# One-hot rows of the tail lists from broadcast row lists, weighted ones on VectorE, and a POOL copy after every sixth gather

## The chip, the cores and the metric

The kernel runs on one core of a Trainium2 chip. The metric is the device time of one execution in microseconds (us); lower is better. The kernel before took a median of 753.49 us over eight runs (747.69 to 759.23).

The core's engines are TensorE (PE in the profile; its weight loads are PEld), VectorE (DVE), ScalarE (ACT), GpSimd (POOL) and SyncE (SP). Each takes its own instructions strictly in order. SP, ACT and POOL also issue DMA transfers; such an issue stands in the same order as the engine's other instructions.

## The reference

Two graph layers over 4096 nodes with 64 features, and a dense 4096 x 4096 matrix `adj` of zeros and ones in which a row holds eight ones on average:

```python
h = relu(layernorm(x))
x = x + layer0(h, adj)
h = relu(layernorm(x))
x = x + layer1(h, adj)
```

Layer 0 takes, for each node i, the mean over its neighbours j of a logarithmic map from i to j on the Poincare ball. The map needs the vectors h[i] and h[j], their norms, the norm of their difference, and an arctanh. A matrix product and an exponential map follow. Layer 1 is `w @ (h @ weight) + bias`, where `w` weighs the last neighbour of a row with 1, the one before it with 1/2, and so on: 0.5 to the power of the number of ones to its right in its row.

## The kernel before, in words

The kernel takes the sparse matrix apart instead of working on all pairs. Its nodes lie in 32 blocks of 128 rows; eight blocks are a quarter.

*The load stage.* SP loads `adj` in halves of a block into `room`; TensorE transposes it (L888), ACT writes it as small numbers into `masks` (L891), and TensorE packs it into words from which VectorE reads the columns of the ones (`pack`, `search`). The first six entries of a row's list, the ELL list, go to `ell_i`. What is left of all rows of a block is gathered into a compact tail list (`tail_split`, `tail_first`, `tail_second`). It holds three columns of 128 entries per block, and of each entry two things: the neighbour's number in `tail_i`, and the row within the block that it belongs to, counted from 1, in `tail_r` (0 for an empty entry). These four functions work per quarter and send their lists through memory on ACT's DMA queue to bring them into another layout.

*The units.* Layer 0 is worked off in 17 units. A unit has the ELL lists of two blocks (12 columns), or the tail lists of two or three blocks (6 or 9 columns), or both (up to 21). Units 0 to 4 have no tail, the last has nothing else; twelve have one. For a unit:

- `fetch` loads the blocks' own rows (`hi`) and, for a tail, the blocks' vectors as three bf16 parts (`hr`), on ACT's queue.
- `gather` has POOL issue one indirect DMA per column (L1139): 128 rows of 65 numbers from `tab_d` into the tile `g`, of which there are two.
- `tail_rows` makes, for a tail, the 0/1 matrix that says which row of its block each entry belongs to. ACT makes it in the orientation "entry by row" with one `Abs` per column (L1156) and one `Relu` (L1163), into `oh`. TensorE transposes it (L1169), and ACT copies it from PSUM into `mt` (L1170). With `mt` as weights and `hr` as data, TensorE selects for each entry its own row's vector (L1178) into a PSUM tile `sel` (and `mi` from the seventh column on).
- `differ` has VectorE subtract (L1192 for ELL, L1208 for the tail) into `d`, and ACT squares the result into `g` (L1222).
- `weigh` sums the squares on VectorE (L1234), after which `g` is free, and works out a weight `r` per entry on VectorE and ACT (L1235 to L1251).
- `total` multiplies the ELL part by `r` and adds it up on VectorE (L1281, L1288). For the tail, ACT scales the columns of `oh` by `r` into `mr` (L1261) and TensorE multiplies `mr` with `d` (L1266), again into a PSUM tile `sel`; `total_tail` adds that to `y` (L1295).

`mt` and `hr` share the memory of `mr`. There is one buffer each of `mr`, `oh`, `d`, of the PSUM tile `sel` and of `mi`, and two of `g` and `hi`.

*The rest.* `middle` finishes layer 0 for a group of blocks and makes the data of layer 1; `collect` has TensorE multiply `masks` with it (L1422, 1024 matmuls) and adds the results to `acc`, on VectorE (L1441, L1445) or through ACT and POOL (L1436, L1438). `write` sends `acc` out. A dense path at the end runs only where a list overflows; it is not entered here.

*What sets the order.* Each call is entered in `plan` with a time in us by `at`, and the times, less the offsets in `EARLY`, become priorities. A scheduler then fixes the order of every engine's instructions by these priorities and by its own account of when each could run; the semaphores are set by it, too. So an instruction need not stand where the program text has it. In `plan`, `tail_rows` is due 6 us after the unit's `gather`, `differ` 7.

Of the kernel before, what the change touches and what calls it, by code (L numbers as in the profile page):

```python
# [19 lines left out]
P = 128  # L20
# [28 lines left out]
QB = 8  # L49
# [7 lines left out]
TB = 3  # L57
MAXT = 3
# [490 lines left out]
def kernel(  # L549
# [61 lines left out]
    ta_d = [dram.tile([P, SUB], F32, name=f"ta_d{q}") for q in range(NQ)]  # L611
    flag_d = dram.tile([1, 1], I32, name="flag_d")
# [3 lines left out]
    with ExitStack() as fast:  # L616
# [67 lines left out]
        tail_i = const.tile([P, NB, TB], I32, name="tail_i")  # L684
        tail_r = const.tile([P, NB, TB], F32, name="tail_r")
# [64 lines left out]
        prep = fast.enter_context(tc.tile_pool(name="prep", bufs=2))  # L750
# [24 lines left out]
        nc.vector.tensor_scalar(pk[:, 1, :], f_e, pd_i.bitcast(F32), None, ALU.mult)  # L775
        row_i = late2[:, 2 * NG : 2 * NG + P].bitcast(I32)
# [39 lines left out]

        def expanded():
# [13 lines left out]
        gp = fast.enter_context(tc.tile_pool(name="gp", bufs=2))  # L831
        blk = fast.enter_context(tc.tile_pool(name="blk", bufs=1))
# [10 lines left out]
        EARLY = {"middle":30,"search":30,"fetch_words":30,"tail_rows":30,"differ":30,"weigh":30,"total":30,"total_tail":30,"ell_lists":30,"tail_split":30,"tail_first":30,"tail_second":30,"gather":30,"fetch":30}  # L843
# [210 lines left out]
        def tail_first(q):  # L1054
# [14 lines left out]
            tac = lst.tile([P, 4, SUB // 4], F32, name="tac")  # L1069
# [9 lines left out]
        def tail_second(q):  # L1079
# [20 lines left out]
            lt = lst.tile([32, REST], F32, name="lt")  # L1100
            nc.vector.transpose(lt, tb)
            lv = lt.rearrange("p (t k b) -> p k b t", t=TB, k=4)
# [9 lines left out]
        def fetch(u):  # L1112
            rb = u["ell"]
            if rb is not None:
                hi = blk2.tile([P, 2, DT], F32, name="hi")
                u["hi"] = hi[:, :, 1:DT]
                nc.scalar.dma_start(out=hi, in_=tab_v[:, rb : rb + 2, :])
            if u["tail"]:
                t0, nt = u["tail"]

                u["mr"] = blk.tile([P, MAXT * TB, P], F32, name="mr")
                half = u["mr"].rearrange("p b c -> p (b c)").bitcast(BF16)
                u["mt"] = half[:, 0 : MAXT * TB * P].rearrange("p (b c) -> p b c", c=P)
                hr = half[:, MAXT * TB * P :][:, 0 : MAXT * 3 * DT]
                u["hr"] = hr = hr.rearrange("p (b c) -> p b c", c=3 * DT)
                nc.scalar.dma_start(out=hr[:, 0:nt, :], in_=hp_d[:, t0 : t0 + nt, :])

        def gather(u):
# [9 lines left out]
            for k, i in enumerate(idx):  # L1138
# [5 lines left out]
                )  # L1144
            u["ns"] = len(idx)

        def tail_rows(u):

            if not u["tail"]:
                return  # L1150
            t0, nt = u["tail"]
            nb = nt * TB
            oh = u["oh"] = blk.tile([P, MAXT * TB, P], BF16, name="oh")

            for k in range(nb):
                nc.scalar.activation(  # L1156
                    oh[:, k, :],
                    row128,
                    AF.Abs,
                    bias=tail_r[:, t0 + k // TB, k % TB : k % TB + 1],  # L1160
                    scale=-1.0,
                )
            nc.scalar.activation(oh[:, 0:nb], oh[:, 0:nb], AF.Relu, bias=1.0, scale=-1.0)  # L1163
            mt, u["sel"] = u["mt"], []
            for k0 in range(0, nb, SEL):
                part = range(k0, min(k0 + SEL, nb))
                mp = ps_m.tile([P, SEL, P], BF16, name="mi")
                for k in part:
                    nc.tensor.transpose(mp[:, k - k0, :], oh[:, k, :], ident_b)  # L1169
                nc.scalar.copy(mt[:, k0 : part.stop], mp[:, 0 : len(part)])  # L1170
# [82 lines left out]
        def total(u):  # L1253
# [3 lines left out]
            if u["tail"]:  # L1257
                t0, nt = u["tail"]
                mr = u["mr"]
# [332 lines left out]
```

## Time and profile before

The profile is one execution, recorded by the hardware.

| | |
|---|---|
| time of the profiled execution | 757.62 us |
| its span, first to last instruction | 755.8 us |
| mean granted TensorE clock | 0.679 of full speed |
| gathers, POOL L1139 | 288, about 1.25 us apart within a train |
| `room` loads from `adj`, SP | 128 of 512 KB |
| `tl_d`, `ta_d` and their loads back, ACT's queue | 40 |

A row of a group names line, engine, operation, the output and input tiles with shapes and how often; then busy us and mean ns of one; then the idle time of the engine just ahead of these instructions, and what ended it. The chain that ended last is followed back from the last instruction, each time to what released it. "Issue" is time in which an engine waited for nothing that the profile shows; "remote", or "another core or an unknown queue", is a wait whose end the profile can put down to none of the core's engines or transfers. A run of gathers with no more than the usual 0.3 us between them is called a train here.

### The profile page before, as it was taken

Reading aid. Unit: us, or ns where it says so; the run is one execution under the profiler, and the core shown is the slowest. Engines: PE = TensorE matmul, PEld = TensorE weight load, DVE = VectorE, ACT = ScalarE, POOL = GpSimd, SP = SyncE. Lnnn points to the kernel's source line nnn. Section 1 sums busy time; section 2 is a strip of 40 time slices with the busy share of each in tenths; the row PEclk is TensorE's granted clock in tenths of the full one; section 3 lists DMA queues with packets and bytes.
Section 4 is the critical chain, followed back from the end, with each engine's and each line's share of the span. In section 5 each row is a group of like instructions: output and inputs, shape, how many; then the busy total and the mean of one; then the engine's idle time right before and its main releaser. Section 6 shows DMA issues by size and latency. Waiting matters only on the chain.

```text
span 755.8 us, 11841 instructions
## 1 busy us (share of the span) xinstructions
PE 395.0 (52%) x4094; PEld 338.3 (45%) x4094; DVE 404.0 (53%) x1557; ACT 345.1 (46%) x791; POOL 351.6 (47%) x423
## 2 busy tenths in 40 slices
PE   3651555624641607655067251442275368979881
PEld 3541444523531506554054241332164167979871
DVE  7750568635691607983179553793623136764520
ACT  6741655725660709955166251442242214565430
POOL 1285414255277260373705364577173712007892
PEclk9865568657775658956556555555556678998996
DMA  8983568746773616876201111221111110000001
GB/s 307 384 317 79 195 212 270 267 140 205 253 283 82 191 23 238 286 253 192 32 16 19 26 34 23 45 37 26 29 27 33 28 16 12 14 10 1 2 27 35
DMA packets 42858, 88.23 MB, mean 117 GB/s; under 512 B 14756, under 2 KB 20388, under 8 KB 42660
## 3 DMA queue, kind: packets, MB, share of 16 engines
q1 hardware_dynamic: 21458, 72.93, 26.9%
q0 software_dynamic: 9504, 10.67, 8.2%
q10 hardware_dynamic: 11826, 3.78, 2.2%
q8 instruction: 34, 0.56, 0.3%
q14 instruction: 36, 0.29, 0.1%
HBM read 83.11 MB, written 4.24 MB: 116 GB/s over the span
## 4 chain that ended last, share of the span: by engine, by line
DVE 23%; PE 21%; another core or an unknown queue 21%; ACT 16%; issue 11%; DMA 4%; ACTq 2%; POOL 1%; DVEq 0%; POOLq 0%; SPq 0%
PE a_ps L1422 9%; ACT mask L891 7%; PE a_ps L888 4%; DVE mask L1412 3%; PE words L917 2%; PE sel L1266 2%; DVE cand L981 1%; DVE tl L1095 1%; DMA room<-in_adj 1%; DVE tb L1093 1%; ACT oh L1156 1%; POOL acc L1438 1%; ACT mr L1261 1%; DMA w_sb<-in_L_gnn_weight 1%
## 5 line engine op out<-in xcount | busy, mean ns | idle before, releaser
L1139 POOL DMA_INDIRECT g<-tab_d,ell_i x192 | 199.6, 1039 | 268.6 <-DVE d L1234 72.3
L891 ACT ACTIVATE mask<-a_ps 128x1024 fp8e5<-128x1024 bf16 x128 | 128.0, 1028 | 111.2 <-remote 73.9
L888 PE MATMUL a_ps<-ident_b,room 128*128 128x128 bf16 x1024 | 103.8, 266 | 59.6 <-ACT mask L891 38.6
L1422 PE MATMUL a_ps<-room,mask 128*128 128x192 bf16 x1024 | 109.6, 259 | 34.2 <-issue 27.6
L888 PEld LDWEIGHTS <-room 128*128 128x128 bf16 x1024 | 90.0, 157 | 66.9 <-issue 66.5
L1139 POOL DMA_INDIRECT g<-tab_d,tail_i x96 | 93.4, 973 | 48.8 <-issue 27.4
L1422 PEld LDWEIGHTS <-mask 128*128 128x128 fp8e5 x1024 | 92.9, 104 | 44.3 <-issue 42.4
L917 PE MATMUL words<-pk,mask 128*128 128x64 bf16 x1024 | 59.3, 216 | 68.3 <-ACT mask L891 43.7
L917 PEld LDWEIGHTS <-mask 128*128 128x128 fp8e5 x1024 | 47.6, 113 | 100.5 <-ACT mask L891 54.7
L981 DVE MAX8 cand<-wsb 128x8 f32<-128x256 f32 x96 | 40.3, 420 | 92.4 <-ACT wsb L928 86.4
L1266 PE MATMUL sel<-d,mr 128*128 128x65 f32 x192 | 41.2, 379 | 23.2 <-issue 19.7
L1266 PEld LDWEIGHTS sel<-d,mr 128*128 128x128 f32 x192 | 39.1, 296 | 27.2 <-issue 21.8
L1438 POOL TENSOR_TENSOR acc<-acc,dg 128x128 f32<-128x128 f32 x60 | 27.8, 464 | 37.8 <-ACT dg L1436 35.7
L1412 DVE TENSOR_TENSOR mask<-mask 128x1024 int16<-128x1024 int16 x60 | 40.5, 674 | 6.6 <-ACT mask L968 6.6
L1261 ACT ACTIVATE mr<-oh,r 128x128 f32<-128x128 bf16 x96 | 29.3, 389 | 21.8 <-DVE r L1251 11.1
L1441 DVE TENSOR_REDUCE wsb<-a_ps 128x128 f32<-128x384 f32 x24 | 13.3, 555 | 45.8 <-remote 29.2
L1438 POOL TENSOR_TENSOR acc<-acc,mr 128x128 f32<-128x128 f32 x60 | 28.6, 477 | 14.8 <-ACT mr L1436 12.9
L1169 PE MATMUL mi<-ident_b,oh 128*128 128x128 bf16 x96 | 12.5, 276 | 39.5 <-issue 22.3
L904 PE MATMUL words<-gn,ones_b 1*128 1x352 bf16 x32 | 12.1, 384 | 38.6 <-ACT cn L931 25.8
L1156 ACT ACTIVATE oh<-row,tail_r 128x128 bf16<-128x128 bf16 x96 | 29.4, 390 | 3.5 <-DVE tail_r L1109 3.4
L1169 PEld LDWEIGHTS <-oh 128*128 128x128 bf16 x96 | 8.5, 122 | 43.3 <-issue 27.1
L1386 PE MATMUL t<-w_sb,room 64*128 64x64 f32 x66 | 17.0, 349 | 19.1 <-DVE room L1405 15.7
(332 smaller groups left out, 769.5 us busy)
## 6 DMA issues: line engine op xcount, KB each, us to landing
room<-in_adj SPq DMA_DIRECT2D x128, 512.0 KB
g<-tab_d,ell_i POOLq DMA_INDIRECT x192
hp_d<-mask SPq DMA_DIRECT2D x1, 1560.0 KB
g<-tab_d,tail_i POOLq DMA_INDIRECT x96
mr<-hp_d ACTq DMA_DIRECT2D x8, 146.2 KB
tab_d<-mask POOLq DMA_DIRECT2D x2, 520.0 KB
hi<-tab_d ACTq DMA_DIRECT2D x16, 65.0 KB
mask<-in_x SPq DMA_DIRECT2D x2, 512.0 KB
```

Of the source, the lines that this page charges most:

```text
L888: nc.tensor.transpose(a_ps[:, k, :], upper[:, e : 2 * HC : 2 * JH], ident_b)
L891: nc.scalar.activation(masks[q][:, j0 : j0 + QB, bass.ts(b, P)], a_ps, AF.Copy, scale=2.0**-ONE, saturate=False,)
L917: nc.tensor.matmul(w, lhsT=masks[q][:, j, bass.ts(b, P)], rhs=pk, start=False, stop=True, skip_group_check=True,)
L981: nc.vector.max(out=top, in_=src)
L1139: nc.gpsimd.indirect_dma_start(out=g[:, k, :], out_offset=None, in_=tab_d, in_offset=bass.IndirectOffsetOnAxis(ap=i, axis=0),)
L1156: nc.scalar.activation(oh[:, k, :], row128, AF.Abs, bias=tail_r[:, t0 + k // TB, k % TB : k % TB + 1], scale=-1.0,)
L1169: nc.tensor.transpose(mp[:, k - k0, :], oh[:, k, :], ident_b)
L1261: nc.scalar.activation(mr[:, k, :], u["oh"][:, k, :], AF.Copy, scale=r[:, e2 + k : e2 + k + 1])
L1266: nc.tensor.matmul(ag[:, k // TB, :], lhsT=mr[:, k, :], rhs=d[:, e2 + k, :], start=(k % TB == 0), stop=(k % TB == TB - 1),)
L1412: nc.vector.tensor_tensor(m[:, :, j, :], m[:, :, j, :], m[:, :, j - 1 if j else JH - 1, :], ALU.add)
L1422: nc.tensor.matmul(o[:, k, 0:W3], lhsT=masks[p][:, b0 + j, bass.ts(2 * n + k, P)], rhs=sup[c][:, j, :], start=(j == 0), stop=(j == nb - 1 ...
L1438: nc.gpsimd.tensor_tensor(ab, ab, ev[:, :, k * D : k * D + D], ALU.add)
```

## The change: what it does

There are three parts.

1. *One-hot rows by comparison.* `tail_second` also turns the entries into row numbers in bf16 and stores them to memory (`tr_d`), four DMAs per quarter on ACT's queue. `fetch_rows` loads a unit's row numbers back, the same numbers to all 128 partitions, on ACT's queue, into `mt`. One VectorE operation (`row_values`) compares each with the partition's own number (`row_p`), in place, which gives the matrix `mt` in the orientation that L1178 needs. The `Abs`, the `Relu`, the transposes and the copies go. `row_values` also holds the selection matmuls. In `plan` it is due about 9 us after the previous unit's `differ` time or once the lists are known, no later than `tail_rows` was; `fetch_rows` 1.5 us ahead of it.
2. *Weighted ones in one operation.* `mr` is made by one VectorE operation per column, which compares `row128` (1 to 128 along the row) with the entry's row number and multiplies by `r`. `oh` goes.
3. *A copy after every sixth gather.* POOL copies one column of the gather that it has just issued into `rest`, which makes it wait until that gather has landed.

The memory is arranged for it: the pool `prep` is closed early, `tac` and `lt` lie in tiles that were there, and `mt`, `hr` and `mr` become tiles of their own.

```diff
+RUN = 6
+    tr_d = [dram.tile([QB, TB, 4, 32], BF16, name=f"tr_d{q}") for q in range(NQ)]
+        nc.vector.tensor_scalar(row_p, part_i, 1, None, ALU.add)
...
+        prep_pool.__exit__(None, None, None)
...
-            tac = lst.tile([P, 4, SUB // 4], F32, name="tac")
+            tac = ti[:, 0:SUB].rearrange("p (k m) -> p k m", k=4)
...
-            lt = lst.tile([32, REST], F32, name="lt")
+            lt = tb_i[:, 0:REST]
             nc.vector.transpose(lt, tb)
+
+            ti = tb.bitcast(I32)
+            tr = tb_i[:, REST:].bitcast(BF16)[:, 0:REST]
+            nc.vector.tensor_copy(ti, tb)
+            nc.vector.tensor_scalar(ti, ti, 12, None, ALU.logical_shift_right)
+            nc.vector.tensor_copy(tr, ti)
+            for k in range(4):
+                nc.scalar.dma_start(
+                    out=tr_d[q][:, :, k, :],
+                    in_=tr[k * QB : (k + 1) * QB, :].rearrange("b (t e) -> b t e", t=TB),
+                )
...
+        def fetch_rows(u):
+
+            t0, nt = u["tail"]
+            u["mt"] = blk.tile([P, MAXT * TB, P], BF16, name="mt")
+            nc.scalar.dma_start(
+                out=u["mt"][:, 0 : nt * TB, :].rearrange("p b c -> p (b c)"),
+                in_=tr_d[t0 // QB][t0 % QB : t0 % QB + nt]
+                .rearrange("b t k e -> (b t k e)")
+                .partition_broadcast(P),
+            )
...
+                if k % RUN == RUN - 1:
+                    nc.gpsimd.tensor_copy(rest[:, 0:1], g[:, k, 0:1])
...
-            for k in range(nb):
-                nc.scalar.activation(
-                    oh[:, k, :],
-                    row128,
-                    AF.Abs,
-                    bias=tail_r[:, t0 + k // TB, k % TB : k % TB + 1],
-                    scale=-1.0,
-                )
-            nc.scalar.activation(oh[:, 0:nb], oh[:, 0:nb], AF.Relu, bias=1.0, scale=-1.0)
             mt, u["sel"] = u["mt"], []
-            for k0 in range(0, nb, SEL):
-                part = range(k0, min(k0 + SEL, nb))
-                mp = ps_m.tile([P, SEL, P], BF16, name="mi")
-                for k in part:
-                    nc.tensor.transpose(mp[:, k - k0, :], oh[:, k, :], ident_b)
-                nc.scalar.copy(mt[:, k0 : part.stop], mp[:, 0 : len(part)])
+            nc.vector.tensor_scalar(mt[:, 0:nb], mt[:, 0:nb], row_p, None, ALU.is_equal)
...
-                    nc.scalar.activation(
-                        mr[:, k, :], u["oh"][:, k, :], AF.Copy, scale=r[:, e2 + k : e2 + k + 1]
+                    nc.vector.tensor_scalar(
+                        mr[:, k, :],
+                        row128,
+                        tail_r[:, t0 + k // TB, k % TB : k % TB + 1],
+                        r[:, e2 + k : e2 + k + 1],
+                        ALU.is_equal,
+                        ALU.mult,
                     )
...
+            if u["tail"]:
+                known = loaded((u["tail"][0] // QB + 1) * QB - 1) + 26.0
+                early = min(max(before + 9.0, known + 2.0), z)
+                at(early - 1.5, fetch_rows, u)
+                at(early, row_values, u)
             u_fetch = z + 3.0
-            at(z, tail_rows, u)
+            before = z
```

## The prediction, made before the changed kernel was run

> **What bounds the kernel now.** No engine does: I read the busy totals first, then the chain that ended last, then a stretch in which the chain names no engine of ours.
>
> ```profile
> PE 395.0 (52%) x4094; PEld 338.3 (45%) x4094; DVE 404.0 (53%) x1557; ACT 345.1 (46%) x791; POOL 351.6 (47%) x423
> DVE 23%; PE 21%; another core or an unknown queue 21%; ACT 16%; issue 11%; DMA 4%; ACTq 2%; POOL 1%; DVEq 0%; POOLq 0%; SPq 0%
> ```
>
> Every engine is about half busy, and a fifth of the chain (20.6% of 755.8 us, 156 us) is on nothing that the profile can name; a further 11% is an engine that waits for nothing shown. The largest such piece, at 262.6 us, cut into windows (columns: length, then busy us and count of PE, PEld, DVE, ACT, POOL, then clock, DMA share, GB/s):
>
> ```profile
> 257.00:262.00 5.00, 3.45 (x53) 2.94 (x53) 4.28 (x25) 3.98 (x12) 3.55 (x4) 0.82 0.93 350
> 262.00:266.00 4.00, 1.13 (x8) 0.71 (x7) 0.41 (x2) 0.64 (x4) 3.06 (x4) 0.50 0.18 31
> 270.00:275.00 5.00, 0.00 (x0) 0.00 (x0) 0.00 (x0) 0.00 (x0) 3.77 (x4) 0.50 0.17 27
> 283.00:287.00 4.00, 2.75 (x36) 2.27 (x36) 2.51 (x12) 3.83 (x7) 0.00 (x0) 0.50 0.72 247
> ```
>
> While POOL issues one gather every 1.25 us, all else stands still; it comes back some 3 us after the last gather. At 561 us, in another train of gathers, the timeline shows how it begins:
>
> ```profile
> 562.34 0.37 PE L1169 MATMUL mi<-ident_b,oh 128*128 128x128 bf16 x2 [0.51 <-issue]
> 563.07 0.27 PE L1169 MATMUL mi<-ident_b,oh 128*128 128x128 bf16 x1 [0.35 <-issue]
> 564.46 0.38 PE L1169 MATMUL mi<-ident_b,oh 128*128 128x128 bf16 x2 [1.13 <-issue]
> 572.24 0.36 DVE L1295 TENSOR_TENSOR y<-y,sel 128x195 f32<-128x195 f32 x1 [15.68 <-remote]
> ```
>
> TensorE starts one instruction per 0.7 or 1.4 us and waits for nothing shown; the addition at L1295 gets its sum 15.7 us late. This begins about 5 us into a train when TensorE is busy (257.5 to 262), later when it has little to do. So a train of gathers starves TensorE, and ACT and VectorE wait for TensorE. POOL in turn waits for them:
>
> ```profile
> POOL g L1139 <- DVE d L1234: 72.3, 4, 25.0
> POOL g L1139 <- DVE u L1235: 52.2, 4, 14.2
> POOL g L1139 <- DVE w L1198: 52.2, 4, 19.8
> POOL g L1139 <- DMA g<-tab_d,ell_i: 1.2, 4, 0.3
> ```
>
> Two gather tiles exist, so a train starts when the unit two back has been reduced. From 313 us on, nine trains are cut off from each other by gaps of 9.4 to 25 us (one of 33.5 before them). These gaps are where the change can pay.
>
> **The change, part by part.** The profiled execution took 757.62 us (span 755.8 and 1.8 around it), 4.1 above the median of 753.49; the sum is made against 757.6 and 4.1 is taken off at the end.
>
> What goes, per unit with a tail (twelve):
>
> ```profile
> L1156 ACT ACTIVATE oh<-row,tail_r 128x128 bf16<-128x128 bf16 x96 | 29.4, 390 | 3.5 <-DVE tail_r L1109 3.4
> L1261 ACT ACTIVATE mr<-oh,r 128x128 f32<-128x128 bf16 x96 | 29.3, 389 | 21.8 <-DVE r L1251 11.1 <-DVE acc L1445 9.5 <-DVE r L1249 0.7
> L1170 ACT COPY mr<-mi 128x768 bf16<-128x768 bf16 (+1 forms) x20 | 13.4, 672 | 24.6 <-PE mi L1169 10.4 <-remote 6.0 <-DVE th_p L738 4.7
> L1163 ACT ACTIVATE oh<-oh 128x1152 bf16<-128x1152 bf16 (+1 forms) x12 | 12.7, 1056 | 22.0 <-PE sel L1266 15.9 <-remote 5.9
> ```
>
> 85 us of ACT and 96 transposes leave. ACT has 400 us idle, so only what stands between a finished train and the next one counts. *Copies L1170*: the selection matmuls wait for them; 13.4/12 = 1.1 us per unit, on the path. *Transposes*: 12.5 us busy in all, 1.0 per unit, but 3.3 us for six of them in the starved stretch above; I take 2.0. *Abs and Relu*: (29.4+12.7)/12 = 3.5 us, mostly beside TensorE's weighted sums, but ahead of the next Square in ACT's order; between 0 and 3.5, I take 0.5, since ACT's idle time before L1156 is 3.5 us in all. *Weighted ones*: nine take 2.73 us on ACT (timeline at 288.8). As one VectorE operation each, they lie between four-in-a-row L940 (0.62 us for four, 128x128: 0.16) and L1445 (0.30): 1.4 to 2.7 us for nine; I take 0.2 each, the shape being L940's: 1.8, so 0.9 gained.
>
> What comes: *comparison* on VectorE, 128x1152 in bf16: at the rate of the cast L823 (2080 in 1.24 us) 0.69, at that of L1192 (768 in 0.945) 1.42; one source as in L823, so 0.7, on the path. *The broadcast of the row lists* (`fetch_rows`): ACT issues it behind `hr`, whose landing buffer TensorE must have left; VectorE's built order has the comparison for unit n+1 ahead of the last part of unit n (before `differ` of one unit, before the reduction of others), so its landing can hold VectorE, with the weights of unit n and the next train behind it. No row shows this transfer; the chain has small loads that end it after 1.5 to 1.7 us and one of 6.5 (`tl<-tl_d` at 247.8). Its issue stands before the Square (1.1 us) that the reduction needs anyway; below 0 us, above 6.5, I take 0.8, the 1.6 less half of it under the Square. *Lists to memory*: sixteen 64-byte-row stores on ACT's queue, at 0.6 us per issue (L1059) 2.4 us per quarter, and three small VectorE operations, under 0.3 each; the tail gathers that need the same lists take over 10 us to issue, which covers both; if that cover fails, 3 us in each of four places, 12 in all. The tile renames (`tac`, `lt`), the pool closed early and `row_p` cost nothing: the same buffers are waited for in the same order, and setup runs beside the first loads.
>
> *The waits.* A POOL copy reads a column of every sixth gather, 48 in all. But the scheduler orders POOL's work, and in the built order most copies stand behind the whole train (18 gathers, then two copies; 12, then two or four; 19, one, 2, two). They do not cut a train into sixes; they add a drain at its end. Behind them waits the next train, and whoever needs it. A copy of one column costs less than L1438's 0.46 us (128x128), and more than nothing; I take 0.2: 0.6 per unit. The landing cannot be over the 10 us that eight gathers take, since reuse of the eight queues never waited over 0.3. In every late gap but one (491.0 to 492.6) POOL waits over 9 us for VectorE anyway, which hides both; 2 us for that one. Without cover: 17 trains by 2 us, 34.
>
> Two rules of the Trainium skill speak against this. SBUF — State Buffer, "SBUF: two separate sides": a VectorE operation in a two-port mode locks GpSimd out of descriptor writing, 620 ns becoming 3100. Our trace's row disagrees so far:
>
> ```profile
> L1139 POOL DMA_INDIRECT g<-tab_d,ell_i x192: 938/944/4098, 35.7 to 595.8; - x192
> ```
>
> Half the gathers are within 6 ns of the shortest, with VectorE 53% busy. By the rule, with two gathers held per unit, I estimate 24 x 2.5 = 60 us more; by the row, none. DMA: Bandwidth & Descriptors, "Anatomy of one DMA", gives about 2 us of fixed completion per gather; by it, all 48 waits in the open would make an estimated 96 us, and in this order few are.
>
> The sum: per late unit -1.1 -2.0 -0.5 -0.9 +0.7 +0.8 = -3.0; nine of them -27. The three earlier tail units lie in the load stage, beside `room` loads and packing: -1 each. Waits +2. Together -28: 757.6 - 28 = 729.6, less 4.1: **726 us**. TensorE must still do some 690 of the 1024 L1422 matmuls after 640 us; their inputs come from these units, so that stage moves forward whole.
>
> **Rivals.** *B, the starving itself shrinks.* 192 fewer TensorE instructions and a drain after every train let TensorE catch up. For: after the 1.6 us break at 491 it ran at full pace for some us. Against: trains stay 18 to 21 long. A quarter of the 156 us: -39, so about 690. *C, nothing moves*: the gaps end with the starved TensorE, not with copies (at 575.7 ACT itself had stood for 18.4 us); the new VectorE work eats the rest: about 752. *D, slower*: VectorE, in order, is held by the broadcast's landing while a finished train waits. For: the built order above. Against: it is issued before the Square. It decides from 0.8 + 3.0 = 3.8 us per unit upward; at 6.5 us it is 9 x 2.7 = 24 slower, 778; I set it at 770.
>
> **Chances.** Forecast 0.50 (its own range 708 to 744), B 0.15, C 0.10, D 0.25. Under 0.5% (3.8 us) a measurement of this kernel can't tell a change. Faster: forecast and B, 0.65; same: C, 0.10; slower: D, 0.25. To leave a tenth out on each side the range runs from B's 690 to 775, just short of D's end.
>
> **What the profile will show.** Right: no transposes by `ident_b,oh`; ACT's busy time near 265 us; weighted ones on VectorE near 0.2 us; the late gaps some 3 us shorter; trains still 18 to 21 long and still starved. Wrong: if the comparison waits for its broadcast by over 3.8 us (D), if "another core" falls well under 20% (B), if gaps stay at 9 to 25 us (C), or if gathers lengthen from 944 ns.

## The result, and the profile after

The changed kernel takes 763.37 us (median of 22 runs, 754.36 to 773.01) where the kernel before takes 753.82 (59 runs, 746.06 to 762.55). Some runs of each kernel are longer than the rest, and with those over 1.5 % above a kernel's fastest left out the ratio is 1.0104, with a 95 % interval of 1.0078 to 1.0130: 1.0 % slower. The profiled execution took 761.86 us (span 760.0), 4.2 us of span more than that of before. It lies a little below its kernel's median, and that of before (757.62 us) a little above, so the two profiles differ by less than the medians.

Busy time of the engines and the shares of the chain that ended last, from the page of the changed kernel:

```profile
PE 394.5 (52%) x3998; PEld 335.5 (44%) x3998; DVE 432.7 (57%) x1678; ACT 266.5 (35%) x567; POOL 359.0 (47%) x467
another core or an unknown queue 24%; PE 23%; DVE 16%; issue 11%; ACT 10%; DMA 9%; POOL 4%; ACTq 3%; SPq 0%; DVEq 0%; POOLq 0%
```

ACT lost 78.6 us of work, as announced, and VectorE got 28.7 more. The share that nothing in the profile can name did not fall: 24 % in place of 21 %. The train that starts at 262 us shows the same picture as that of before (windows; columns: length, then busy us and count of PE, PEld, DVE, ACT, POOL, then clock, DMA share, GB/s):

```profile
262.00:267.00 5.00, 5.00 (x59) 4.08 (x56) 4.22 (x22) 3.13 (x9) 3.85 (x4) 0.50 0.60 214
271.00:279.00 8.00, 2.10 (x13) 1.08 (x14) 0.00 (x0) 0.78 (x2) 6.17 (x7) 0.50 0.19 29
279.00:284.00 5.00, 1.09 (x4) 0.41 (x3) 0.00 (x0) 0.00 (x0) 3.78 (x5) 0.50 0.18 27
```

TensorE's own timeline in it, in place of the transposes that were caught in the train before:

```profile
268.38 0.19 PE L1187 MATMUL mi<-hr,mt 128*128 128x65 bf16 x1 [0.51 <-issue]
276.17 0.43 PE L896 MATMUL a_ps<-ident_b,room 128*128 128x128 bf16 x2 [1.14 <-issue]
281.06 0.27 PE L896 MATMUL a_ps<-ident_b,room 128*128 128x128 bf16 x1 [1.14 <-issue]
```

Five microseconds in which TensorE is busy throughout (at a granted clock of 0.50), then one instruction per 0.7 to 1.4 us: the starving is untouched. What POOL waits for at the head of its trains did change (waits on POOL; total us, times, longest):

```profile
POOL g L1164 <- DVE d L1243: 89.3, 6, 24.9
POOL g L1164 <- DVE w L1207: 31.2, 2, 17.3
POOL g L1164 <- DVE d L1036: 24.6, 1, 24.6
POOL g L1164 <- DVE tb L1101: 18.2, 1, 18.2
POOL g L1164 <- DVE tb L1113: 13.8, 1, 13.8
POOL rest L1171 <- DMA g<-tab_d,tail_i: 4.1, 3, 1.6
```

It is VectorE in every large row, as before, but `tb` and `d` at L1036 are not sums of a unit: they are steps of making the row lists of a quarter, and L1113 is one of the change's own. By the timeline of POOL one train of before (gathers 120 to 140, 313.2 to 342.4) is now two, because the second quarter's lists were not there for its tail:

```profile
309.54 1.03 POOL L1164 DMA_INDIRECT g<-tab_d,ell_i  x1 [24.85 <-DVE d L1243]
351.21 0.97 POOL L1164 DMA_INDIRECT g<-tab_d,tail_i  x1 [24.56 <-DVE d L1036]
369.39 0.97 POOL L1164 DMA_INDIRECT g<-tab_d,ell_i  x1 [5.78 <-DVE d L1243]
```

The last of those lists is written at 351.7 us, against 324.8 in the kernel before. Up to that point VectorE has 202.4 us of work in place of 187.6, of which the new operations are 7.3 us, and 149.3 us of idle time in place of 137.2; so most of these 27 us are idle time and other work that stands in front, not the new operations. Up to 415 us the changed kernel falls 12 us behind (gather 162 at 414.7 and 402.7), then makes that up in shorter gaps: the gap of 14.3 us that the kernel before has ahead of 546 us is gone, and the gathers from 495.9 to 579.0 us follow each other with breaks of 1.7 us at most. The last train ends at 636.4 and 635.6. All gaps between trains from 280 us on add up to 137 us, against 140. So the forecast's 27 us came down to 3, and the stage after the last gather is 3.4 us longer (123.6 and 120.2).

The new operations on VectorE, by line (count, then shortest/median/longest ns, first and last start), and what the comparison waited for:

```profile
L1270 DVE TENSOR_SCALAR mr<-row,tail_r,r x96: 320/338/611, 292.2 to 703.1; 128x128 f32<-128x128 bf16 x96
L1179 DVE TENSOR_SCALAR mt<-mt,row_p x12: 411/512/520, 254.2 to 648.7; 128x1152 bf16<-128x1152 bf16 x8, 128x768 bf16<-128x768 bf16 x4
  DMA mt<-tr_d: 18.2, 6
```

Waits on ACT that a transfer on its own queue ended (total us, times, longest):

```profile
ACT mask L899 <- DMA tr_d<-tl: 6.2, 1, 6.2
ACT q__4777 L1250 <- DMA tr_d<-tl: 5.9, 1, 5.9
ACT u L1255 <- DMA tr_d<-tl: 3.5, 1, 3.5
```

And a reading that the experiments turned up: VectorE's busy time from the start to the end of the second group's layer, the addition `acc<-acc,room` at L1359 (L1373 after the change), whose second occurrence starts at 539.7 us before and 547.5 after. First the kernel before, then the changed one (windows, columns as above; the third pair is VectorE):

```profile
0.00:539.70 539.70, 244.10 (x2648) 202.30 (x2648) 313.16 (x1245) 263.15 (x564) 251.34 (x255) 0.64 0.49 156
```

```profile
0.00:547.50 547.50, 248.46 (x2612) 202.48 (x2612) 330.55 (x1319) 214.97 (x424) 253.78 (x286) 0.62 0.50 158
```

17.4 us more work for VectorE, 9.6 us less idle time (547.50 - 330.55 = 216.95 against 226.54), and the layer 7.8 us later. After it TensorE has nearly all of the 1024 closing matmuls to do, and both kernels need about as long for that: 216.1 us from that point to the end of the span before, 212.5 after.

### The profile page after: what moved, and what is told of

It reads as the page before. It is cut to its first block, busy times and chain, and to the rows that moved or that the text cites. A ratio compares the mean times of both kernels' runs of the same rounds, so it can differ in the third digit from the quotient of the medians.

```text
span 760.0 us, 11672 instructions
## 1 busy us (share of the span) xinstructions
PE 394.5 (52%) x3998; PEld 335.5 (44%) x3998; DVE 432.7 (57%) x1678; ACT 266.5 (35%) x567; POOL 359.0 (47%) x467
## 3 DMA queue, kind: packets, MB, share of 16 engines
q1 hardware_dynamic: 21458, 72.93, 26.8%
## 4 chain that ended last, share of the span: by engine, by line
another core or an unknown queue 24%; PE 23%; DVE 16%; issue 11%; ACT 10%; DMA 9%; POOL 4%; ACTq 3%; SPq 0%; DVEq 0%; POOLq 0%
PE a_ps L1436 8%; ACT mask L899 5%; PE a_ps L896 5%; DMA room<-in_adj 4%; PE words L925 3%; PE sel L1280 2%; DMA mt<-tr_d 2%; POOL g L1164 2%; POOL acc L1452 2%; DVE mask L1426 1%; DMA tab_d<-mask 1%; DMA w_sb<-in_L_gnn_weight 1%; DMA tl_d<-tl 1%; DVE d L1243 1%
## 5 line engine op out<-in xcount | busy, mean ns | idle before, releaser
L1164 POOL DMA_INDIRECT g<-tab_d,ell_i x192 | 195.7, 1019 | 237.7 <-DVE d L1243 89.3
L896 PE MATMUL a_ps<-ident_b,room 128*128 128x128 bf16 x1024 | 107.0, 268 | 45.8 <-issue 20.5
L925 PEld LDWEIGHTS <-mask 128*128 128x128 fp8e5 x1024 | 50.6, 115 | 161.0 <-issue 110.8
L925 PE MATMUL words<-pk,mask 128*128 128x64 bf16 x1024 | 64.3, 221 | 93.0 <-issue 52.2
L1436 PEld LDWEIGHTS <-mask 128*128 128x128 fp8e5 x1024 | 94.0, 105 | 34.4 <-issue 29.7
L1231 ACT ACTIVATE g<-d 128x1344 f32<-128x1344 f32 (+3 forms) x17 | 18.9, 1110 | 65.5 <-DVE w L1220 42.9
L1187 PEld LDWEIGHTS <-mt 128*128 128x128 bf16 x288 | 16.4, 122 | 33.5 <-issue 31.8
L1309 DVE TENSOR_TENSOR y<-y,sel 128x195 f32<-128x195 f32 (+1 forms) x12 | 3.9, 326 | 46.9 <-remote 41.4
L1270 DVE TENSOR_SCALAR mr<-row,tail_r,r 128x128 f32<-128x128 bf16 x96 | 27.0, 363 | 2.2 <-POOL acc L1452 2.1
L1317 ACT COPY room<-o 64x512 f32<-64x512 f32 (+1 forms) x18 | 9.5, 527 | 50.9 <-remote 25.7
L1187 PE MATMUL sel<-hr,mt 128*128 128x65 bf16 x216 | 12.1, 226 | 28.2 <-DVE y L1309 21.0
```

What stands on the lines that cost most here:

```text
L896: nc.tensor.transpose(a_ps[:, k, :], upper[:, e : 2 * HC : 2 * JH], ident_b)
L925: nc.tensor.matmul(w, lhsT=masks[q][:, j, bass.ts(b, P)], rhs=pk, start=False, stop=True, skip_group_check=True,)
L1164: nc.gpsimd.indirect_dma_start(out=g[:, k, :], out_offset=None, in_=tab_d, in_offset=bass.IndirectOffsetOnAxis(ap=i, axis=0),)
L1187: nc.tensor.matmul(sel[:, k - k0, :], lhsT=mt[:, k, :], rhs=u["hr"][:, k // TB, n * DT : n * DT + DT], start=(n == 0), stop=(n == 2),)
L1231: nc.scalar.activation(g[:, 0:ns, 1:DT], d[:, 0:ns, 0:D], AF.Square)
L1270: nc.vector.tensor_scalar(mr[:, k, :], row128, tail_r[:, t0 + k // TB, k % TB : k % TB + 1], r[:, e2 + k : e2 + k + 1], ALU.is_equal, ALU. ...
```

## The experiments

The 18 runs were made in five sessions, each on one chip. In all of them the kernel before took 564 to 567 us (medians), not 754; every ratio below is against its runs on the same chip. Here the trains do not starve TensorE: the chain of the kernel before has no piece of "another core" at all, and POOL issues its last 168 gathers between 229.8 and 458.6 us with gaps of 3 us at most. Its chain there (run e8_before_again):

```profile
POOL 24%; DVE 20%; PE 17%; DMA 15%; ACT 10%; issue 10%; ACTq 1%; DVEq 0%; SPq 0%; POOLq 0%
```

So these runs can tell what each part of the change does to the engines' work and order, but not what it does to starved trains. They use the names of theories as they came up: W, the POOL copies and their landing; V, VectorE's added work; O, the built order, which every edit shifts; E, the early place of the comparison in the plan; S, transfers on ACT's in-order queue; T, TensorE as the bound of the closing stage however it starts.

The whole table first. Busy and idle are VectorE's up to the end of the second group's layer, at the time in the fifth column; the last column is from there to the end of the span (windows of each run's trace; idle is the difference). The ratio is of many runs, the other columns are of one trace each: that of e8 took 561.92 us where its chip's median is 564.99, that of e3 is the shortest of its six runs, that of e18 the longest of its twelve. With no work added the idle time already differs by 8 us (e18 against e8), and the last column runs from 171.6 to 184.9 us, so a single difference of that size says little.

| run | ratio to before, 95 % | busy | idle | layer at | to the end |
|---|---|---|---|---|---|
| e8 before, again | (1) | 309.9 | 71.2 | 381.1 | 179.0 |
| e13 plan constant | 0.9992 [0.9964, 1.0021] | 309.8 | 73.5 | 383.3 | 179.8 |
| e14 column copy, per unit | 0.9876 [0.9822, 0.9929] | 310.7 | 68.0 | 378.7 | 178.0 |
| e18 column copy, per tail | 1.0030 [0.9998, 1.0063] | 309.8 | 79.3 | 389.1 | 179.8 |
| e15 mask sums later | 1.0048 [1.0022, 1.0075] | 304.4 | 81.4 | 385.8 | 180.2 |
| e2 POOL copies alone | 1.0123 [1.0071, 1.0176] | 309.9 | 78.7 | 388.6 | 183.5 |
| e9 stores of lists alone | 1.0122 [1.0063, 1.0180] | 312.0 | 79.4 | 391.4 | 178.1 |
| e3 weighted ones alone | 1.0142 [1.0087, 1.0196] | 327.0 | 67.0 | 394.0 | 171.6 |
| e17 weighted ones twice | 1.0408 [1.0363, 1.0452] | 338.9 | 69.3 | 408.2 | 179.2 |
| e4 rows alone | 1.0330 [1.0280, 1.0381] | 318.8 | 83.1 | 401.9 | 173.7 |
| e12 rows alone, late | 1.0306 [1.0238, 1.0374] | 319.1 | 84.7 | 403.8 | 177.9 |
| e11 rows alone, by SyncE | 1.0193 [1.0138, 1.0247] | 319.6 | 79.6 | 399.2 | 174.8 |
| e5 whole change | 1.0282 [1.0252, 1.0311] | 329.5 | 69.7 | 399.2 | 183.3 |
| e1 whole, no copies | 1.0273 [1.0222, 1.0325] | 328.3 | 72.0 | 400.3 | 178.5 |
| e6 whole, own tile | 1.0321 [1.0271, 1.0371] | 328.7 | 73.1 | 401.8 | 181.0 |
| e7 whole, own tile, no copies | 1.0264 [1.0224, 1.0304] | 328.4 | 72.3 | 400.7 | 182.2 |
| e10 whole, lists by SyncE | 1.0361 [1.0311, 1.0411] | 330.9 | 74.1 | 405.0 | 177.1 |
| e16 whole, mask sums later | 1.0456 [1.0406, 1.0506] | 326.4 | 76.6 | 403.0 | 184.9 |

**The parts one by one.** e1_no_copies takes the two lines `if k % RUN == RUN - 1:` and `nc.gpsimd.tensor_copy(rest[:, 0:1], g[:, k, 0:1])` out of the changed kernel; e2_copies_alone puts them into the kernel before.

> The changed kernel without the 48 POOL copies; all else as changed. Theory W (the waits cost it: each train of gathers ends with a drain of its landing, 17 trains by 1 to 2 us): 17 to 34 us below the changed kernel, ratio to the kernel before 0.965 to 0.99. Theory V (the work put on VectorE and the landing of the broadcast cost it, the copies nothing): 1.005 to 1.015, as the changed kernel. Theory O (each edit lets the scheduler set another order, and the length of single gaps between trains comes out by that order more than by the edit's cost): anything from 0.985 to 1.015, with one or two gaps changed by 10 us and the rest the same.

> The kernel before with the 48 POOL copies alone. Theory W: 1.01 to 1.045 times the kernel before. Theory V: 1.000, at most 1.003 (one train of 17 was not behind a longer wait: 2 us). Theory O: 0.985 to 1.015, and not equal to the difference between the changed kernel with and without copies.

e3_ones_alone is the kernel before with

```diff
-                    nc.scalar.activation(
-                        mr[:, k, :], u["oh"][:, k, :], AF.Copy, scale=r[:, e2 + k : e2 + k + 1]
-                    )
+                    nc.vector.tensor_scalar(
+                        mr[:, k, :], row128, tail_r[:, t0 + k // TB, k % TB : k % TB + 1],
+                        r[:, e2 + k : e2 + k + 1], ALU.is_equal, ALU.mult,
+                    )
```

> The kernel before with the weighted ones alone moved to one VectorE operation each; the ones are still built on ACT, since the transposes read them. 96 x 0.36 us = 35 us more on VectorE, 29 us less on ACT; on the path nine take 9 x 0.363 = 3.3 us in place of 2.7. Theory V: nine units by 0.6, plus what waits on VectorE behind them: 5 to 20 us slower, 1.007 to 1.025. Theory W: 1.00 to 1.005. Theory O: 0.985 to 1.015, without relation to the 0.6 us.

e4_rows_alone is the changed kernel without copies, and with the weighted ones on ACT, in place in one tile:

```diff
+                nc.scalar.activation(
+                    mr[:, k, :], row128, AF.Abs,
+                    bias=tail_r[:, t0 + k // TB, k % TB : k % TB + 1], scale=-1.0,
+                )
+            nc.scalar.activation(mr[:, 0:nb], mr[:, 0:nb], AF.Relu, bias=1.0, scale=-1.0)
...
-                    nc.vector.tensor_scalar(
-                        mr[:, k, :], row128, tail_r[:, t0 + k // TB, k % TB : k % TB + 1],
-                        r[:, e2 + k : e2 + k + 1], ALU.is_equal, ALU.mult,
-                    )
+                    nc.scalar.activation(
+                        mr[:, k, :], mr[:, k, :], AF.Copy, scale=r[:, e2 + k : e2 + k + 1]
+                    )
```

> Row lists by broadcast and the comparison on VectorE, without copies; the weighted ones stay on ACT (distance, one minus it, and the weight, in place in one tile). So the transposes and their copies are gone, and the comparison and its landing are in. The forecast's sum for this part: -1.1 -2.0 +0.7 +0.8 = -1.6 per late unit, with the measured 0.5 and 1.5 for the last two -1.1: 10 to 14 us faster, 0.98 to 0.987. Theory V with the landing as cause: 1.00 to 1.01. Theory O: 0.985 to 1.015.

Without copies the whole change stays at 1.027, so W falls as its cause; alone they cost 1.2 %, though the copies wait only 15.8 us for landings in all, and what waits for a copy is one gather, by 0.5 us, and one Square on ACT, by 4.7. Rows alone, the part for which I had forecast a gain, is the costliest by itself at 3.3 %. It is not the broadcast and the comparison alone, though: its ones are built in the single fp32 tile `mr`, and ACT's Abs waits there 10.6 us in all for the weighted sums that still read it. The sum of the three parts, 1.2 + 1.4 + 3.3 = 5.9 %, is twice the whole: they do not add.

**The whole, and a wait of 26.8 us.** In the changed kernel the last unit has its weights at 496.3 us and writes its weighted ones at 523.2: the tile `mr`, no longer taken early by the load of `hr`, is held by a sum of `collect` that waits for a layer. VectorE's timeline (run e5_whole):

```profile
496.28 0.15 DVE L1260 TENSOR_TENSOR r<-r,rj 128x6 f32<-128x6 f32 x1
523.22 2.29 DVE L1270 TENSOR_SCALAR mr<-row,tail_r,r 128x128 f32<-128x128 bf16 x6 [2.12 <-POOL acc L1452]
527.47 0.29 DVE L1309 TENSOR_TENSOR y<-y,sel 128x130 f32<-128x130 f32 x1 [0.58 <-PE sel L1280]
```

The same 26.8 us stand in the profile of the result (674.3 to 701.1). e6_own_tile takes the wait away, and e7_own_tile_no_copies the copies too:

```diff
-                mr = blk.tile([P, MAXT * TB, P], F32, name="mr")
+                if e2:
+                    mr = blk.tile([P, MAXT * TB, P], F32, name="mr")
+                else:
+                    mr = d.rearrange("p s c -> p (s c)")[:, ns * DT : ns * DT + ns * P]
+                    mr = mr.rearrange("p (b c) -> p b c", c=P)
```

> The whole change on the same chip and beside the same runs of before as the three that follow. Theory O (single places of the built order decide; here the last unit's weighted ones, which wait 26.8 us for a tile that they share with the sums of collect): 1.02 to 1.04 where trains of gathers do not starve TensorE (the kernel before took 566 us on the chip of the first four runs), 1.01 where they do (754 us). Theory W adds 7 us for the copies to the 1.027 measured without them: 1.04.

> The whole change, but the last unit, which gathers no neighbour lists, puts its six weighted ones into the free end of its own tile of differences in place of the tile that collect also uses. Theory O: the ones follow the weights within 1 us in place of 26.8, the last tail sum comes some 25 us earlier, and the stage after the last gather is 8 to 12 us shorter (113 to 103 us on the fast chip, 124 to 116 on the other): 1.0 to 2 % below the whole change. Theory W or V: the stage after the last gather is bound by TensorE's 720 to 790 remaining matmuls at 7 per us, the wait is beside it, and the time moves by less than 3 us (0.5 %).

> As the last, and without the POOL copies. Theory O: 1.000 to 1.01 times the kernel before on the fast chip (1.027 less 10 us of 566 is 1.009), and 7 us below the kernel with copies. Theory V: 1.02 to 1.03, as without copies and with the shared tile.

> The kernel before, for its trace on this chip. If trains starve TensorE here: time 754, joint stalls of TensorE, ACT and VectorE of 100 us in all, another core or an unknown queue near 20 % of the chain. If not: 566, under 2 %, and gathers back to back from 250 to 460 us, with the last tail sum some 30 us after the last gather.

The wait went, in e6_own_tile:

```profile
494.50 0.15 DVE L1260 TENSOR_TENSOR r<-r,rj 128x6 f32<-128x6 f32 x1
494.69 1.63 DVE L1274 TENSOR_SCALAR d<-row,tail_r,r 128x128 f32<-128x128 bf16 x6
499.73 0.29 DVE L1313 TENSOR_TENSOR y<-y,sel 128x130 f32<-128x130 f32 x1 [0.89 <-PE sel L1284]
```

The last tail sum came 28 us earlier, and the kernel not a microsecond: 1.032 against 1.028, and 113.0 us after the last gather against 113.3. TensorE has 694 and 726 closing matmuls left there (589 in the kernel before, which needs 101.4 us) and works through them at seven per us whatever the last unit does. My theory fell; the largest single new wait of the changed kernel costs nothing. What does differ is how much TensorE has left, and that follows from when the second group's layer lets it start: 381 us before, 399 after.

**Transfers on ACT's queue.** In e4 ACT stands 17.1 us ahead of the logarithm of a finished train, with four stores of the lists ahead of it in its order that wait for VectorE (waits on ACT, e4_rows_alone):

```profile
ACT q__5452 L1266 <- DMA tr_d<-tl: 17.1, 1, 17.1
```

This is not what the stores cost. The logarithm's own input, from VectorE, is done at 400.6 us, and the logarithm starts at 402.5:

```profile
400.47 0.16 DVE L1265 SCALAR_TENSOR_TENSOR q__5452<-q__5452,u 128x21 f32<-128x21 f32 x1
402.45 0.22 ACT L1266 ACTIVATE q__5452<-q__5452 128x21 f32<-128x21 f32 x1 [17.09 <-DMA tr_d<-tl]
```

The stores held it for 1.8 us; the rest of the wait it would have had without them.

e9_stores_alone gives the kernel before the three VectorE operations and four stores per quarter (`tr_d`), which nobody reads. e10_lists_by_sp and e11_rows_by_sp replace `nc.scalar.dma_start` by `nc.sync.dma_start` in those stores and in `fetch_rows`, in the whole change and in rows alone. e12_rows_late tests the place in the plan instead, in rows alone:

```diff
-                at(early - 1.5, fetch_rows, u)
-                at(early, row_values, u)
+                at(z - 1.5, fetch_rows, u)
+                at(z, row_values, u)
```

> The kernel before, which also writes the row lists to memory (three small VectorE operations and four stores on ACT's queue per quarter); nothing reads them. Theory S (ACT, in order, stands at the stores, which wait for VectorE's lists and take 0.69 us each to issue; what is behind them, Sign and Square of finished trains among it, comes late): ACT shows idle stretches of 3 to 17 us ended by these stores, and the time is 1.01 to 1.02. Theory E (it is the early place of the fetch and the comparison in the plan) and theory V (VectorE's own work): 1.000 to 1.004; 16 x 0.69 us of issue are beside other work.

> The whole change (1.028 here), with the stores of the row lists and the broadcast loads issued by SyncE in place of ACT. Theory S: ACT's issues fall from 47 to 31 us, its waits for these transfers go, the second quarter's lists come some 10 us earlier (256 to 246 us) and the ratio falls to 1.00 to 1.015. Theories E and V: 1.02 to 1.03. A rival to S: SyncE stands at the stores too, with the loads of the adjacency behind it until some 250 us; then the load stage lengthens and it is 1.03 or more.

> Row lists by broadcast alone, ones on ACT, no copies (1.033 with ACT as issuer), with both transfers issued by SyncE. Theory S: 0.985 to 1.01; the forecast's gain of 1 us per late unit can show. Theory E: 1.025 to 1.035.

> Row lists by broadcast alone, ones on ACT, no copies (1.033), with fetch and comparison planned where tail_rows stood (6 us after the start of the unit's train) in place of 9 us after the unit before. Theory E: 1.00 to 1.015. Theory S: 1.025 to 1.035.

The place in the plan is not it: 1.031. Issued by SyncE, rows alone improve from 1.033 to 1.019, so some 1.4 of the 3.3 % go with the issuer; but the whole change gets worse, 1.036. SyncE's waits show why it is no remedy there (e10_lists_by_sp): it stands at the broadcast loads, with the loads of the layers behind them.

```profile
SPq L1146 <- PE sel L1187: 105.7, 8, 21.6
SPq L1146 <- DVE mt L1179: 18.0, 5, 4.8
```

**Is it only the built order?** Three parts, each alone, had cost 1.2 to 1.4 %. e13_plan_shift changes `SH = 6.0` to 6.5 in the kernel before; e14_one_column adds `nc.vector.tensor_copy(idle[:, 0:1], r[:, 0:1])` at the start of `total`, e18_one_column_tail the same kind of copy at the end of `total_tail`. e15_steps_later and e16_change_steps_later hold the mask sums of a quarter back behind its lists, by a one-element operation that reads the lists, in the kernel before and in the changed one:

```diff
+            m = masks[q].bitcast(I16).rearrange("p (h j) i -> p h j i", h=NH)[0:1, 0, 1, 0:1]
+            nc.vector.scalar_tensor_tensor(m, li[0:1, 0, 0:1], 0.0, m, ALU.mult, ALU.add)
...
-            t = loaded(p * QB + QB - 1) + 12.0
+            t = loaded(p * QB + QB - 1) + 28.0
```

> The kernel before with one constant of the plan changed (the offset of a unit's sums from the start of its train, 6.5 in place of 6.0): the same instructions, in an order that may differ. Theory O (any change of the built order costs some per cent, and the 1.2 % of a part is nothing but that): 1.01 or more. Theory V (VectorE's work and waits before the second group's layer set when the closing stage begins): 0.997 to 1.005.

> The kernel before with one copy of a single column on VectorE per unit, 17 in all, which nobody reads: some 17 x 0.15 = 2.5 us of VectorE. Theory O: 1.01 or more, like the other small edits. Theory V: 1.5 us of it lie before the second group's layer: 1.000 to 1.005.

> The kernel before, with the mask sums (L1412, 0.67 us each) of a quarter held back until the lists of that quarter are done; in the kernel before some nine of them stand between the rounds that select the second quarter's lists. Theory V: those lists come some 6 us earlier (241 to 235 us), the second group's layer and the first matmuls of its part of the closing stage with them, and the time is 3 to 8 us lower, 0.985 to 0.995. Theory T (the closing stage has TensorE as its bound wherever it starts, and starts when the load stage and the gathers let it): 0.997 to 1.003. Theory O: 1.01.

> The whole change with the mask sums held back in the same way. Theory V: its second lists come 10 us earlier (256 to 246), and it is 1.01 to 1.02 in place of 1.028. Theory T: 1.025 to 1.03.

> The kernel before with one copy of a single column on VectorE at another place, after the sum of each of the twelve tails; nobody reads it. A second sample of what the built order alone does, beside 0.999 for the shifted plan constant and 0.988 for the first column copy. Theory O at its full size: 1.01 or more, or 0.99 or less. Theory V: 0.995 to 1.005.

An edit with no work to speak of gives -1.2, -0.1 and +0.3 %. So O is real: 1.2 % in one of three samples, to the fast side. Three samples don't give its full reach, nor show a loss of 1 %; I take it as about 1 % either way. By that the 1.2 % of the copies and of the stores and the 1.4 % of the ones cannot be told from it, the 1.9 to 4.6 % of the kernels with rows by broadcast can. One of these accidents, e14, is the fastest kernel of the study (559.79 us beside 566.62), and says nothing of the change. The mask sums, held back, brought the second lists to 235.0 us as expected, from 240.8, and the layer no nearer (385.8): VectorE's work ahead of it fell by 5.5 us and its idle time rose by 10 (by 8 in e18, which takes nothing away). Taking that work away did not pay (1.0048), and V in the form "all that VectorE does there counts" fell with it. In the changed kernel the second lists came 6.5 us earlier too (249.5), and the time rose to 1.046; its layer came 3.8 us later than in e5, for which I have no cause.

**Does added work come through?** e17_ones_twice writes each weighted one of e3 twice (`for k in [*range(nt * TB)] * 2`).

> The kernel before with the weighted ones on VectorE (1.014), and each of them written twice. Up to the end of the second group's layer VectorE had 310.6 us of work and 70.6 us idle in the kernel before, 327.7 and 66.3 with the ones. Theory V (work given to VectorE ahead of that layer comes through in full): some 15 us more of work, idle time unchanged, the layer done near 409 us in place of 394, and a time of 1.035 to 1.045. Theory O (the 1.2 to 1.4 % of a part is the built order alone) or a cover for VectorE's work: 1.00 to 1.02, with VectorE's idle time down by 10 us or more.

Yes, and nearly in full. VectorE's time up to the second group's layer, in the kernel before, with the ones once (e3), and twice (e17):

```profile
0.00:381.10 381.10, 235.44 (x2648) 196.19 (x2648) 309.87 (x1245) 260.92 (x564) 248.63 (x244) 0.73 0.66 220
```

```profile
0.00:394.00 394.00, 244.92 (x2684) 202.26 (x2684) 327.01 (x1318) 252.10 (x528) 259.82 (x253) 0.69 0.66 213
```

```profile
0.00:408.20 408.20, 248.56 (x2684) 205.37 (x2684) 338.88 (x1369) 250.04 (x519) 265.23 (x252) 0.68 0.62 206
```

Work goes 309.9, 327.0, 338.9; idle time stays at 71, 67 and 69; the layer comes at 381, 394 and 408 us; and the kernel takes 0, 1.4 and 4.1 % more. From the start of the long run of gathers to that layer VectorE is busy 88 % of the time in the kernel before, 91 % in e3 and 94 % in e17 (133.5 of 151.3, 152.0 of 166.8 and 159.9 of 170.1 us), so there is little idle time to hide in. A second way in is not excluded: the gathers themselves take 303.6, 306.3 and 313.8 us in sum, so that in e17 the last one ends 18 us later than in the kernel before, 10 of them by longer gathers. The whole change looks like the same case:

```profile
0.00:399.20 399.20, 237.53 (x2612) 197.63 (x2612) 329.52 (x1320) 212.88 (x424) 265.41 (x286) 0.68 0.66 217
```

19.6 us more work than before, idle time 1.5 us less, the layer 18.1 us later, the span 22 us longer. VectorE is busy 91 % of the time from the start of the long run of gathers to the layer. ACT has 48 us less to do up to the same point and TensorE 36 instructions fewer, and neither shows in the time.

What stays open: what else the broadcast of the rows costs. In e4, e11 and e12 about half of the delay is VectorE's work (+9 to +10 us) and half its idle time (+8 to +14 us, where e18 has +8 without any change of work); with ACT as issuer part of that can be the stores, and the single tile `mr` of these three kernels another part; no run separates them. And why trains starve TensorE in the runs of the result and in none of these. Versions that throttle the trains in earnest were therefore not tried.

## Why the prediction was wrong, point by point

The forecast was 726 us, faster; it took 763, inside the stated range of 690 to 775 and on the side given a chance of 0.25, but not by the mechanism that was named for it.

- *The step that failed* is in the sum "per late unit -1.1 -2.0 -0.5 -0.9 +0.7 +0.8 = -3.0; nine of them -27": it follows one unit from its train to the next and charges VectorE's new work only where it lies on that way. The forecast had found that POOL waits for VectorE at every large row and that VectorE runs in order, and yet gave its 29 new us no place behind which other work queues. They stand ahead of the lists of the next quarter and of the second group's layer, and 1010 of the 1024 closing matmuls come after that layer, in both kernels. Doubling the ones showed it, where trains do not starve TensorE: 17 and 12 us of work, 13 and 14 us of delay. In the profile of the result 9.6 of 17.4 us were swallowed by idle time that starved trains leave to VectorE, which fits the smaller loss there (1.0 against 2.8 %); that the same link holds there is read from its two traces, not tried. It is not the whole of it: of the 27 us by which the second quarter's lists come late there, the new operations are 7.3.
- *What was taken away* went as announced: no transposes, ACT at 266.5 us (said: near 265). It was worth 3 us of gaps in place of 27. By the rows shown, before and after, VectorE ends the large waits at the heads of trains; whether the copies, transposes and ones by ACT stood on the way to those ends was not tried where trains starve TensorE. Where they don't, 48 us less on ACT do not show in the time.
- *The weighted ones* were said to take 0.2 us each, by the row of L940. They take 0.34, one every 0.27: nine in 2.4 us (292.2 to 294.6) against 2.73 on ACT. The gain of 0.9 was 0.3. The nearer row was the other end of the bound, L1445 with 0.30; the range of 1.4 to 2.7 us for nine held it.
- *The comparison* cost 0.51 us (said 0.7), its landing 18.2 us in 6 waits, 1.5 per unit (said 0.8, bounds 0 to 6.5). As a mean that is below the 3.8 us of rival D, but one wait of the six took 11.1 us, beyond the bound, and D's sign did show there. ACT, which issues the load, had itself stood 19.9 us:

```profile
482.97 0.33 ACTq L1146 DMA_DIRECT2D mt<-tr_d  x1
483.34 0.58 ACT L1317 COPY room<-o 64x512 f32<-64x512 f32 x1 [19.91 <-remote]
486.20 0.52 DVE L1179 TENSOR_SCALAR mt<-mt,row_p 128x1152 bf16<-128x1152 bf16 x1 [11.12 <-DMA mt<-tr_d]
```

  The train had ended at 479.5 us, and the gap after it is 16.4 us, where the kernel before has 13.3 at the same place. So D cost some 3 us there; the other five waits took 1.9 us or less. The 6.5 us of the bound were read from a store (`tl_d<-tl`), not from a load as the forecast has it.
- *Lists to memory* were put at nothing, covered by the tail gathers, 12 us if not. The cover was named on the wrong queue: behind the stores on ACT's queue stand its own logarithms and mask copies, and ACT stood 15.6 us there (6.2, 5.9 and 3.5). What that cost is less: VectorE gave the two logarithms their inputs only 2.2 and 2.7 us before they started. Run alone, the stores gave 1.2 %, which the order's own reach doesn't let me call theirs.
- *The copies* were right: they drain the end of a train, nobody waits, and without them the whole change was no faster. There are 44 of them, not 48; they took 0.19 us at the median (said 0.2) and waited 1.6 us at most.
- *The stage after 640 us moves as a whole*, the forecast said. It did not: it starts 0.8 us later and is 3.4 us longer, with some 790 closing matmuls left in place of 710.
- *Nine late units* were charged with 3 us each, but one of the breaks between the nine late trains is the 1.6 us at 491 us, in which there was no 3 us to win.
- *Rival C*, nothing moves, came nearest: gaps unchanged, the new VectorE work on top. It was priced at 752, no change, since the new work was taken to eat no more than the forecast gains.
- *The lock rule.* By SBUF — State Buffer of the Trainium skill, "SBUF: two separate sides", an estimated 60 us more was the price if VectorE's modes hold up descriptor writing. The forecast read the median of the gathers as evidence against the rule. The median is the same after the change, 944 ns:

```profile
L1164 POOL DMA_INDIRECT g<-tab_d,ell_i x192: 940/944/3379, 35.2 to 603.2; - x192
```

  But a median can't show what befalls one gather in eight. In the kernel before 35 of the 288 gathers took over 1100 ns, and 34 of these overlap a `TENSOR_TENSOR` on VectorE; of the 171 gathers that overlap none, one took as long. After the change it is 28 of 30. One such gather of before, and the next one:

```profile
125.79 0.68 DVE L1412 TENSOR_TENSOR mask<-mask 128x1024 int16<-128x1024 int16 x1
125.91 1.38 POOL L1139 DMA_INDIRECT g<-tab_d,ell_i  x1 [0.30 <-issue]
127.59 0.94 POOL L1139 DMA_INDIRECT g<-tab_d,ell_i  x1 [0.30 <-issue]
```

  So gathers take longer beside certain operations of VectorE, and the trace does not speak against the rule; whether its lock is the reason, no run here shows. Only the price of 60 us did not come: all gathers over 960 ns together lose 21 us against 944 ns each before and 18 us after, and of the 19 gathers that overlap the new ones of L1270 a single one took over 1100 ns, beside a `TENSOR_TENSOR` too.
- *The landing.* What DMA: Bandwidth & Descriptors of the Trainium skill, "Anatomy of one DMA", says of a fixed completion of about 2 us agrees with what the copies show: the last gather of a train starts at 323.57 us and its landing releases a copy at 326.46, 2.9 us later, with 0.94 of that the gather's own.

## What to carry to other kernels

Work that moves from an idle engine to the engine that the others wait for must be charged in full at first, and excused only where idle time of that engine, on the way to the work that sets the end, can be named. Where a scheduler orders a program, run a few edits that do nothing before believing a part worth one per cent; here three of them moved the time by -1.2, -0.1 and +0.3 %. A long new wait is no cost until something shows that its end is waited for: 26.8 us of one were removed for nothing, and of 17.1 us on ACT only 1.8 were due to the transfer that ended them. And a median says nothing of what befalls a few instructions; sort the long ones out and look at what ran beside them.

## What was not expected of the hardware

The kernel before takes 754 us in the runs of the result and 564 to 567 us in the five sessions of the experiments, with the same instructions. The difference is in the trains of indirect gathers: in the first, TensorE falls to one instruction per 0.7 to 1.4 us some 5 us into a train, and the engines that wait for it stand; in the others it does not, and POOL goes on at one gather per 1.36 us from 230 to 459 us. A gather itself takes the same 944 ns (median) in both. No run here shows the cause, nor whether it lies in the chip.
